# Attention before a mixture of experts on one core: the first pair of heads assembled by 0/1 matmuls, seven PSUM banks in rotation, the first four pairs worked by halves of the queries, and embeddings moved into the loop

## The chip, the core and the metric

The kernel runs on one core of a Trainium2 chip. A core has a matrix engine (TensorE, PE in the profile, with its weight loads as PEld), VectorE (DVE), ScalarE (ACT), GpSimd (POOL), and queues that issue transfers for its 16 DMA engines; here nearly all go through SyncE (SP). Each engine works its own instructions in order and waits on semaphores for the others. SBUF is the on-chip memory of 128 partitions, PSUM the accumulators of PE: eight banks of 128 x 512 four-byte numbers. The metric is the time of one execution on the device in microseconds (us), lower is better. A time shown for a kernel is the median of its runs.

## The reference

Input is `x` of 4 batches, 1024 tokens and 256 channels, in 16 heads of 16. What matters here is the attention:

```python
q_mag, k_mag = softplus(x @ wq.T), softplus(x @ wk.T)          # by head
q_embed = [q_mag * cos(qp), q_mag * sin(qp)]                   # 32 numbers for each token and head
k_embed = [k_mag * cos(kp), k_mag * sin(kp)]                   # kp: position angles + a bias for each head and channel
scores  = q_embed @ k_embed.T / sqrt(16)
out     = softmax(scores) @ v                                  # then @ wo.T
x       = layernorm(x + out)
x       = layernorm(x + moe(x))                                # 8 experts, the best 2 for each token
```

## The kernel before, in words

**Units.** The heads are cut into two groups `f` of eight, and worked by pairs of heads: 8 pairs for each batch, 32 in all, numbered through as `u`. A pair has eight steps, one for each tile of 128 keys, so there are 256 steps in the loop (L970 to L1018). "Pair 4" below is the first pair of group 1 of batch 0, at step 32.

**A step.** For the pair in work it makes the key scores `st` (keys on partitions, queries along the row) for both heads and all 1024 queries, four matmuls into two PSUM tiles of two banks (`key_scores`, L728); adds minus the query's maximum by four matmuls of two rows with ones (L743); takes exponentials into `pt` on ACT, two instructions of 128 x 1024 (L750); and multiplies the exponentials of the step before by the values, 16 matmuls into `av` (L764). Column 16 of the values is one, so `av` holds the sums too. For the next pair it makes four score tiles `s` the other way round (queries on partitions; `score_half`, L692 to L705) and DVE takes each one's row maximum into `nm`. A pair needs 32 of these. In step 6 of a pair the next pair's maxima are split in two parts (`max_parts`, L711 to L713, DVE), in step 7 they are turned into rows (`max_rows`, L719: four transposes on PE, a copy `mt` on ACT, L721). Extra work is set beside the steps by the table `todo`.

**Embeddings.** `embedding` (L350 to L416) makes 512 tokens of q or k for one group: two matmuls, softplus in three ACT instructions, two products with a table of cosines and sines, and a split of each product into a rounded part and the rest (`parts`, fp32r and its remainder), so that a score from both parts is as good as fp32. The fast form does products and remainders on DVE and the copies on ACT; the slow form does them on POOL (L390 to L405) and reads its table from DRAM. The result goes to DRAM in four writes (L413), because a pair's score matmul wants it in another order of partitions: 32 rows of q part 1, part 1, part 2, part 2 against k part 1, part 2, part 1, part 2, for one head. `load_qk` (L418 to L436) reads it back so: 12 transfers of a pair, four of q and two of k for each of the two heads.

**Tables.** `tab0` holds the angles' cosines and sines (`cs`) and the key table of group 0 (`kt0`). The key table of group 1 is made of `cs` by `second_key_table` (L225 to L235: four ACT copies with a scale, two POOL sums) and stored to DRAM for later batches and for group 1.

**Buffers.** The pool `big` has three buffers of 16 KB a partition: `twice` (weights, read until `once` has copied them), `tab0`, and the pairs' `qk`, which take these over when they are free. The pool tag `parts` has two buffers. `bank()` hands out PSUM: in the loop three single banks, before the loop and in the tail five in rotation, the three and one of the two banks of each `st` tile:

```python
free_banks[0] = (free_banks[0] + 1) % 5
if free_banks[0] > 2:
    return ps_st.tile([P, 2, HS], F32, tag="st", name=name)[:, 0, :]
```

**Before the loop** (L908 to L967, an order written out by hand): the fast embeddings of group 0 in halves of the tokens (k0, q0, k1, q1), each written and loaded back as pair 0 (q's through POOL's queue); the values of group 0; the load of pair 1; table stores; then all 32 score tiles of pair 0, with the two q embeddings of group 1, the values of group 1 and the second key table among them; `max_parts`, `max_rows`. In the loop, step 0 holds eight scores of pair 1 after its exponentials, every later step four; the two k embeddings of group 1 start in steps 2 and 4. At the start of a pair's first step the pair after the next is loaded.

Every SP transfer and every engine's order is as the program gives it; what waits for what follows from the tiles: an instruction waits for the last readers of a buffer that its tile takes over.

## Time and profile before

| | us |
|---|---|
| median of 3 runs (1452.09, 1455.23, 1455.70) | 1455.23 |
| profiled execution | 1455.47 |
| its span, first to last instruction | 1453.6 |
| start of the first exponentials of step 0 | 62.12 |
| steps 0 to 31 (to pair 4's first exponentials, 186.41) | 124.29 |
| PE busy from 0 to 62.12 | 40.91 |
| PE busy from 62.12 to 186.41 | 123.77 |
| PE busy from 186.41 to 1110 (923.59) | 904.29 |
| PE busy from 1110 to 1160 (the attention's tail) | 17.31 |
| PE busy from 1160 to the end (293.60, experts) | 281.41 |

A line of the profile names the engine, the line of the kernel, the operation and the tiles (output <- inputs), and in square brackets how long the engine had been idle and what ended that. Matmul ends are modelled, so a start-to-start distance says more than a duration. "PEclk" and the column after POOL in a table by windows is the clock that the chip granted to PE, 1.00 being full.

### The profile page before, as it was taken

The numbers are of one execution on the slowest core, as the hardware profiler recorded it, in microseconds if no ns is written. First come the engines' busy times: TensorE is split into PE (matmuls) and PEld (weight loads), VectorE is DVE, ScalarE is ACT, GpSimd is POOL, SyncE is SP. The second block draws the span as 40 slices with busy tenths as digits, with TensorE's granted clock in tenths as the row PEclk, the third lists the DMA queues.
The fourth block names the chain that finished last, engine by engine and source line by source line (L and its number), as shares of the span: only waits on it lengthen the run. The fifth ranks groups of instructions, "written<-read, shape, count | busy, mean of one in ns | idle before, by whom it ended". The sixth has DMA issues, their size and how long they took to land. (4 is left out here: it accounts for less than half of the span.)

```text
span 1453.6 us, 24361 instructions
## 1 busy us (share of the span) xinstructions
PE 1367.7 (94%) x9314; PEld 859.4 (59%) x9314; DVE 921.3 (63%) x1990; ACT 727.5 (50%) x944; POOL 411.2 (28%) x436
## 2 busy tenths in 40 slices
PE   5899999999999999999999999999996399999996
PEld 3455555655665565555555555555543277777775
DVE  7767766667877766787767677887644433333334
ACT  5365666565566556546674654655553122222221
POOL 5640043340002637000064530000210414444542
PEclk8899999999999999999999999999998599999998
DMA  7956367373444646454465352224210436433211
GB/s 240 261 177 173 100 188 205 87 228 107 126 120 113 213 133 180 121 151 102 129 185 181 105 176 74 63 63 118 90 64 0 139 112 212 115 120 131 73 44 43
DMA packets 107315, 191.23 MB, mean 132 GB/s; under 512 B 19633, under 2 KB 56178, under 8 KB 107072
## 3 DMA queue, kind: packets, MB, share of 16 engines
q1 hardware_dynamic: 96192, 167.80, 39.7%
q0 software_dynamic: 9888, 20.01, 4.5%
q10 hardware_dynamic: 1120, 1.87, 0.4%
q8 instruction: 73, 1.20, 0.4%
q14 instruction: 42, 0.34, 0.1%
HBM read 119.32 MB, written 73.63 MB: 133 GB/s over the span
## 5 line engine op out<-in xcount | busy, mean ns | idle before, releaser
L705 DVE TENSOR_REDUCE nm<-s 128x1 f32<-128x512 f32 x1024 | 644.8, 684 | 230.4 <-PE s L701 212.6
L750 ACT ACTIVATE pt<-st 128x1024 f32<-128x1024 f32 x512 | 496.3, 1021 | 393.7 <-PE st L743 378.9
L701 PE MATMUL s<-qk 128*128 128x512 f32 x1024 | 391.5, 441 | 25.6 <-DVE nm L705 14.5
L728 PE MATMUL st<-qk 128*128 128x512 f32 x1024 | 308.4, 401 | 3.5 <-ACT pt L750 3.4
L764 PE MATMUL av<-pt,va 128*32 128x256 f32 x4096 | 275.5, 386 | 0.5 <-ACT pt L750 0.5
L701 PEld LDWEIGHTS s<-qk 128*128 128x128 f32 x1024 | 180.2, 191 | 138.3 <-DVE nm L705 62.4
L728 PEld LDWEIGHTS st<-qk 128*128 128x128 f32 x1024 | 183.3, 189 | 67.1 <-ACT pt L750 32.7
L764 PEld LDWEIGHTS av<-pt,va 128*32 128x32 f32 x4096 | 107.1, 109 | 107.8 <-issue 62.4
L646 POOL DMA_INDIRECT slots_in<-held,scatter_idx x64 | 62.7, 980 | 304.4 <-DVE scatter_idx L644 226.4
L390 POOL TENSOR_TENSOR soft_q<-y_q,soft_q 128x512 f32<-128x512 f32 x14 | 17.9, 1282 | 447.3 <-ACT soft_q L386 447.2
L1249 PE MATMUL op<-w,h 128*128 128x256 f32 x640 | 144.1, 379 | 0.0
L1230 PE MATMUL hp<-slots_t,w 128*128 128x320 f32 x512 | 139.9, 434 | 0.0
L743 PE MATMUL st<-mt,ones_r 2*128 2x512 f32 x1024 | 129.6, 495 | 0.7 <-ACT mt L721 0.7
L1249 PEld LDWEIGHTS op<-w,h 128*128 128x128 f32 x640 | 119.4, 190 | 15.9
L1230 PEld LDWEIGHTS hp<-slots_t,w 128*128 128x128 f32 x512 | 97.7, 191 | 40.0 <-ACT slots_t L1083 0.3
L743 PEld LDWEIGHTS st<-mt,ones_r 2*128 2x128 f32 x1024 | 49.0, 181 | 89.5 <-issue 88.1
L1237 ACT ACTIVATE h<-hp,b_sb 128x640 f32<-128x640 f32 x64 | 50.8, 794 | 86.6 <-PE hp L1230 73.3
L1264 DVE TENSOR_TENSOR o<-op,b_sb 128x256 f32<-128x256 f32 x35 | 14.9, 425 | 93.3 <-PE op L1249 88.9
L1265 ACT ACTIVATE o<-o,w 128x256 f32<-128x256 f32 x35 | 17.8, 507 | 103.1 <-issue 71.9
L1267 POOL DMA_INDIRECT y_rank<-o,rows x35 | 35.9, 1025 | 98.4 <-ACT slots_t L1083 42.2
L1191 POOL DMA_INDIRECT out_dram<-row,rows x40 | 41.0, 1025 | 44.6 <-DVE row L1146 14.3
L396 POOL TENSOR_TENSOR e_k<-soft_k,tab_k 128x512 f32<-128x512 f32 x28 | 35.4, 1286 | 46.3 <-DMA tab_k<-table 45.8
(210 smaller groups left out, 1030.6 us busy)
## 6 DMA issues: line engine op xcount, KB each, us to landing
qk<-embed_q SPq DMA_DIRECT2D x248, 128.0 KB
qk<-embed_k SPq DMA_DIRECT2D x124, 256.0 KB
embed_k<-parts_k SPq DMA_DIRECT2D x64, 256.0 KB
w<-in_w_dram SPq DMA_DIRECT2D x16, 1024.0 KB
embed_q<-parts_q SPq DMA_DIRECT2D x56, 256.0 KB
y_rank<-zero SPq DMA_DIRECT2D x8, 1024.0 KB
tab_k<-table SPq DMA_DIRECT2D x14, 512.0 KB
tab_q<-table SPq DMA_DIRECT2D x12, 512.0 KB
```

Of the source, the lines that this page charges most:

```text
L646: nc.gpsimd.indirect_dma_start(out=scatter_views[2 * t + k], out_offset=bass.IndirectOffsetOnAxis(ap=scatter_idx[:, k, t : t + 1], axis=0) ...
L701: nc.tensor.matmul(ps, qk[:, 2 * h, lo : lo + P], qk[:, 2 * h + 1, j * HS : (j + 1) * HS], start=True, stop=True,)
L705: nc.vector.tensor_reduce(nms[u][:, j, i, s : s + 1], ps, AX.X, ALU.max, negate=True)
L728: nc.tensor.matmul(ps[:, f, :], qk[:, 2 * h + 1, c * P : (c + 1) * P], qk[:, 2 * h, f * HS : (f + 1) * HS], start=True, stop=False,)
L743: nc.tensor.matmul(tiles[h][:, f, :], ones_r[rows, :], mts[u][rows, :], start=False, stop=True,)
L750: nc.scalar.activation(pt, tiles[h], AF.Exp)
L764: nc.tensor.matmul(av[32 * s : 32 * (s + 1), cols], va[f][:, c, 2 * p + h, :], pt[h][:, s // 2, cols], start=(c == 0 and n == 0), stop=(c ...
L1191: nc.gpsimd.indirect_dma_start(out=out_views[t], out_offset=bass.IndirectOffsetOnAxis(ap=to[:, 0, t : t + 1], axis=0), in_=row[:, t, :], i ...
L1230: nc.tensor.matmul(ps[:, i, 0:half], w1_sb[:, k, c * P : (c + 1) * P], s_t[:, k, i * half : (i + 1) * half], start=(k == 0), stop=(k == KC ...
L1237: nc.scalar.activation(h_t[:, c, :].rearrange("p (i n) -> p i n", i=2), ps[:, :, 0:half], AF.Gelu, bias=b1_sb[:, e, c : c + 1],)
L1249: nc.tensor.matmul(ps, h_t[:, c, t * P : (t + 1) * P], w2_sb[:, c, :], start=(c == 0), stop=(c == HC - 1),)
L1267: nc.gpsimd.indirect_dma_start(out=y_views[e * ST + t], out_offset=bass.IndirectOffsetOnAxis(ap=to[:, 1, t : t + 1], axis=0), in_=o_sb, in ...
```

## The change

1. *Rows by matmul.* POOL makes `picks`, matrices of zeros and ones. `move_first` puts pair 0's rows in place with them: for q and k, each head and each half of the tokens, four matmuls that add both parts into their places in one PSUM tile, and an ACT copy into `qk_0`. `load_qk` for pair 0 is gone; the writes of the embeddings to DRAM stay, all on SP. The k1 and q1 parts lie in buffers of `pt`; q1 is made in the slow form.
2. *Seven banks.* Rotating work takes the three single banks and both banks of each `st` tile.
3. *Halves.* The four pairs of batch 0, group 0 are worked as eight units of four steps, each for half of the queries; a step then takes two tiles of keys for 512 queries. Before the loop only the 16 scores of the first half are made. A list `ahead` spreads the scores of later units: 6 in step 0, 5 in each of steps 1 to 18, then 4. `max_parts` and `max_rows` come once for each unit, and so do `av`'s copy and its six collecting transfers.
4. *Staged embeddings.* All four embeddings of batch 0, group 1 start in the loop, in steps 3, 7, 11 and 15, with products, split and writes in the steps after. Values of group 1: one half before the loop, one in step 5. The second key table is made in pieces in steps 0, 1, 8 and 9, in buffers of `parts` instead of `pt`. Pair 4's load moves from step 16 to step 19. `nm` has three buffers instead of two.

```diff
+        picks = p1.tile([P, 2, 2, 13, HD], F32R, tag="os", name="picks")
+        for h in range(2):
+            pick = p2.tile([P, 2, 13, HD], F32, tag="y", name=f"pick_{h}")
+            nc.gpsimd.memset(pick, 0.0)
+            for w, (first, apart) in enumerate(((5, 2), (3, 4))):
+                blocks = pick[:, w, first : first + apart + 1 : apart, :]
+                nc.gpsimd.affine_select(
+                    out=blocks, in_=blocks, compare_op=ALU.not_equal, fill=1.0, base=-h,
+                    pattern=[[0, 2], [-FH, HD]], channel_multiplier=1,
+                )
+            nc.gpsimd.tensor_copy(picks[:, h], pick)
...
         def second_key_table(h):
 
             cols = halves[h]
-            a = p4.tile([P, 2, HS], F32, tag="pt", name=f"kta_{h}")
-            kt = p4.tile([P, 2, HS], F32, tag="pt", name=f"kt_{h}")
+            both = p2.tile([P, 2, 2, HS], F32, tag="parts", name=f"kt_{h}")
+            a, kt = both[:, 0], both[:, 1]
             for i, c in enumerate((nb4, sb4)):
                 nc.scalar.activation(a[:, i, :], cs[:, 1 - i, cols], AF.Copy, scale=c[:, 1:2])
                 nc.scalar.activation(kt[:, i, :], cs[:, i, cols], AF.Copy, scale=cb4[:, 1:2])
-            for i in range(2):
                 nc.gpsimd.tensor_tensor(kt[:, i, :], kt[:, i, :], a[:, i, :], ALU.add)
+                if i == 0:
+                    yield
...
-                free_banks[0] = (free_banks[0] + 1) % 5
-                if free_banks[0] > 2:
-                    return ps_st.tile([P, 2, HS], F32, tag="st", name=name)[:, 0, :]
+                free_banks[0] = (free_banks[0] + 1) % 7
+                n = free_banks[0] - 3
+                if n >= 0:
+                    if n % 2 == 0:
+                        two_banks[0] = ps_st.tile([P, 2, HS], F32, tag="st", name=name)
+                    return two_banks[0][:, n % 2, :]
...
+            if apart:
+                parts = [
+                    p4.tile([P, 2, HS], F32R, tag="pt", name=f"parts_{name}_{p}") for p in range(2)
+                ]
+            else:
+                both = p2.tile([P, 2, 2, HS], F32R, tag="parts", name=f"parts_{name}")
+                parts = [both[:, 0], both[:, 1]]
             for i in range(2):
                 if fast:
-                    nc.scalar.copy(parts[:, 0, i, :], e[:, i, :])
+                    nc.scalar.copy(parts[0][:, i, :], e[:, i, :])
                 else:
-                    nc.gpsimd.tensor_copy(parts[:, 0, i, :], e[:, i, :])
+                    nc.gpsimd.tensor_copy(parts[0][:, i, :], e[:, i, :])
             for i in range(2):
-                fine.tensor_tensor(
-                    parts[:, 1, i, :], e[:, i, :], parts[:, 0, i, :], ALU.subtract
-                )
+                fine.tensor_tensor(parts[1][:, i, :], e[:, i, :], parts[0][:, i, :], ALU.subtract)
+            if made is not None:
+                made[w, h] = parts
...
-            by = nc.gpsimd if fast and w == "q" else nc.sync
             for p in range(2):
                 for i in range(2):
-                    by.dma_start(
+                    nc.sync.dma_start(
                         to[2 * p + i, :, :, cols].rearrange("d m s -> (d m) s"),
-                        parts.bitcast(F32)[:, p, i, :],
+                        parts[p].bitcast(F32)[:, i, :],
...
+        def move_first(w, cols, parts):
+
+
+            if 0 not in qks:
+                qks[0] = big.tile([P, 4, S], F32R, tag="big", name="qk_0")
+            k = w == "k"
+            for h in range(2):
+                ps = bank(f"rows_{w}_{h}_{cols.start}", True)
+                for p in range(2):
+                    for c in range(2):
+
+                        at = c + (2 if k else 4) * p
+                        first = (3 if k else 5) - at
+                        nc.tensor.matmul(
+                            ps,
+                            picks[:, h, int(k), first : first + 8, :].rearrange("p b d -> p (b d)"),
+                            parts[p][:, c, :],
+                            start=(p == 0 and c == 0),
+                            stop=(p == 1 and c == 1),
+                        )
+                yield
+                nc.scalar.copy(qks[0][:, 2 * h + k, cols], ps)
...
+        units = []
+        starts, lasting = [], []
+        for i in range(B * NU):
+            for h in range(2) if i < NU // NF else (None,):
+                starts.append(starts[-1] + lasting[-1] if units else 0)
+                units.append((i, *divmod(i // (NU // NF), NF), i % (NU // NF), h))
+                lasting.append(NT if h is None else NT // 2)
+        NS = starts[-1] + lasting[-1]
+        step_of = [(w, c) for w in range(len(units)) for c in range(lasting[w])]
...
+            i, _, _, _, half = units[w]
+            qk = qks[i]
+
+            i, s = divmod(k, 4 if half is None else 2)
+            h = s % 2
+            if w not in nms:
+                nms[w] = small.tile([P, 2, 4, 4], F32, tag="nm", name=f"nm_{w}", bufs=3)
+            lo = HS * (s // 2 if half is None else half) + P * i
+            ps = bank(f"s_{w}_{k}_{j}", rotate)
...
+                h, q, k = (t, x, c) if half is None else (x, half, 2 * c + t)
...
+                        to, k, e = slice(n * DIM, (n + 1) * DIM), c, pt[h][:, q]
+                        e = e[:, to]
...
+                        to, k, e = slice(0, DIM), 2 * c + n, pt[n][:, h]
...
-                if b == 0 and n > 1:
-                    staged(0, ((0, 2), (0, 4))[n - 2], 2, embedding, 0, 1, w, h)
+                if b == 0:
+                    staged(0, ((0, 3), (0, 7), (1, 3), (1, 7))[n], 1, embedding, 0, 1, w, h)
...
+        ahead = [[] for _ in range(NS)]
+        items, due, may = [], [], []
+        for w in range(1, len(units)):
+            rows = range(16 if units[w][4] is None else 8)
+            items += [(w, k, j) for k in rows for j in range(2)]
+            due.append((starts[w] - 2, len(items)))
+
+            before = [starts[v] for v in range(w) if units[v][0] == units[w][0] - 1]
+            may.append((max(0, min(before, default=1) - 1), len(items)))
+        given = 0
+        for n in range(NS):
+            n_items = max([-((given - i) // (d - n + 1)) for d, i in due if d >= n], default=0)
+            most = max(i for first, i in may if first <= n)
+            ahead[n] = items[given : min(given + n_items, most)]
+            given += len(ahead[n])
...
+                    0, 0, w, h, fast=(w, h) != ("q", 1), tab=cs if w == "q" else kt0,
+                    pauses=(KC - 1,), rotate=True, apart=h == 1, made=made,
...
+            for work in (q0, k0, q0, k0, k1, q0, q1):
                 run(work)
+            mk0, mq0 = moving("k", 0), moving("q", 0)
+            key_table(1)
+            for work in (k1, mk0, mq0, mk0, mq0, mk0, mq0, mk0, mq0):
                 run(work)
+            for i in range(2):
+                score_half(0, 2 * i, 0, True)
+            for work in (k1, q1, k0, q0):
                 run(work)
+            for i in range(2, 4):
+                score_half(0, 2 * i, 0, True)
+            values(0, 0, 0, rotate=True)
+            for i in range(4):
+                score_half(0, 2 * i + 1, 0, True)
+            mk1 = moving("k", 1)
+            for work in (mk1, mk1, mk1, mk1, k1):
                 run(work)
+            for i in range(4):
+                score_half(0, 2 * i, 1, True)
+            values(0, 0, 1, rotate=True)
+            for i in range(4):
+                score_half(0, 2 * i + 1, 1, True)
+            run(q1)
+            values(0, 1, 0, rotate=True)
+            max_parts(0)
+            max_rows(0, rotate=True)
+            mq1 = moving("q", 1)
+            for work in (mq1, mq1, mq1, mq1, q1):
+                run(work)
...
-            works = [embedding(0, 1, "q", h, tab=cs, pauses=(0, 1)) for h in range(2)]
-            vals = [values_in_two(0, 1, h) for h in range(2)]
-            beside = {n: (run, works[0]) for n in (3, 5, 6, 11, 17)}
-            beside |= {n: (run, vals[i]) for n, i in ((8, 0), (10, 0), (14, 1), (16, 1))}
-            beside |= {n: (second_key_table, h) for n, h in ((1, 0), (12, 1))}
-            beside |= {n: (run, works[1]) for n in (20, 22, 23)}
...
+        for h in range(2):
+            pieces = second_key_table(h)
+            for c in range(2):
+                at(0, h, c, run, pieces)
+        at(0, 0, 5, values, 0, 1, 1)
...
+                if n % NT == 0 and n != 2 * NT or n == 2 * NT + 3:
+                    i = n // NT + 2
+                    if i < B * NU:
+                        load_qk(i)
...
+                items = [(score_half, *x) for x in ahead[n]]
+                first, third, fourth, rest = items[:2], items[2:3], items[3:4], items[4:]
+                if third_last:
+                    third, fourth = [], third + fourth
...
+                if n + 2 in starts:
+                    max_parts(starts.index(n + 2))
+                if n + 1 in starts:
+                    max_rows(starts.index(n + 1))
```

## The prediction

> **What bounds the kernel now.** First the page: engine shares, and the slices of TensorE (PE) with the clock that it was granted.
>
> ```profile
> PE 1367.7 (94%) x9314; PEld 859.4 (59%) x9314; DVE 921.3 (63%) x1990; ACT 727.5 (50%) x944; POOL 411.2 (28%) x436
> ...
> PE   5899999999999999999999999999996399999996
> ...
> PEclk8899999999999999999999999999998599999998
> ```
>
> PE is full from the third slice of 36 us up to the tail of the attention. Time can be won by less PE work, or in the two places where PE is not full: the start, and about 1,110 to 1,160 us, which the change touches only through the bank order. So next the start, by windows (busy time of PE, PEld, DVE, ACT, POOL; then granted clock, share of the DMA engines, GB/s):
>
> ```profile
> 20.00:30.00 10.00, 1.95 (x18) 1.76 (x16) 9.93 (x19) 7.69 (x14) 6.74 (x14) 0.76 0.79 266
> 30.00:40.00 10.00, 7.71 (x13) 3.70 (x13) 5.00 (x12) 2.43 (x5) 5.60 (x11) 0.56 0.90 298
> ...
> 50.00:60.00 10.00, 6.05 (x18) 2.79 (x16) 8.62 (x15) 2.44 (x4) 9.79 (x10) 0.97 0.67 249
> 60.00:70.00 10.00, 9.32 (x25) 5.14 (x24) 6.79 (x12) 2.52 (x3) 1.54 (x2) 0.52 1.02 291
> ```
>
> PE is nearly empty from 20 to 30 us; from 50 to 60 DVE leads. The waits from 0 to 90 us (total, times, longest) say on what:
>
> ```profile
> DVE nm L705 <- PE s L701: 18.7, 17, 3.3
> ...
> PE s L701 <- DMA qk<-embed_q: 9.9, 2, 8.5
> ```
>
> The timeline places them:
>
> ```profile
> 30.41 0.77 PE L701 MATMUL s<-qk 128*128 128x512 f32 x1 [8.46 <-DMA qk<-embed_q]
> ...
> 59.18 1.03 PE L719 MATMUL mp<-ident,m 128*128 128x128 f32 x4 [3.13 <-DVE m L713]
> 60.25 0.59 ACT L721 CAST mt<-mp 128x512 fp32r<-128x512 f32 x1 [6.19 <-PE mp L719]
> ...
> 62.12 1.94 ACT L750 ACTIVATE pt<-st 128x1024 f32<-128x1024 f32 x2 [1.28 <-PE st L743]
> ...
> 106.89 1.94 ACT L750 ACTIVATE pt<-st 128x1024 f32<-128x1024 f32 x2 [1.55 <-PE st L743]
> 110.38 1.94 ACT L750 ACTIVATE pt<-st 128x1024 f32<-128x1024 f32 x2 [1.55 <-PE st L743]
> ```
>
> The first score waits 8.46 us for the embedding's way through DRAM; 32 scores and maxima follow; the first exponentials of the loop start at 62.12 us. Then a step takes 3.49 us (110.38 - 106.89), with PE never idle. Steps 0 to 31, the part that the change rebuilds, start at 62.12 and end where pair 4's first exponentials start, 186.41: 124.29 us.
>
> **The way up to the first exponentials.** Removed: 24 loads of pair 0, and the eight POOL issues of q's writes, which move to SP behind k's. No score waits for those. Added on PE: 32 matmuls of the size of a score (0.23 us apart at full clock in the steady steps), about 7.4 us in all, half of them where PE now stands idle; on ACT eight copies of 128x512 at 0.59 (L345's and L721's rows). POOL's masks (two fills, four selects, two copies) lie in its idle time between 12.7 and 19.4 us. I followed the new order of instructions with these rows: k's first split ends at 20.8, 1.5 us later than now, because its Abs waits for DVE's copy of an x tile that lies in the same PSUM tile (seven banks are three tiles and two tiles of two banks, and a wait is by tile); q's ends at 22.1; rows are copied at 22.7, 23.4, 25.2 and 26.1; the first score is at 26.2 instead of 30.4. Sixteen maxima at 0.62 to 0.68 instead of 32, with the half embeddings, the values and the shared tiles between them, put the last at 44.1; maxima in parts 1.8 (L711 to L713 from 57.33 to 59.13) to 45.9; transposes, copy and ones as now (59.18 to 62.12, 2.9), with waits for a shared tile and the last four row matmuls between: 51.3 at full clock. **Gain: 62.1 - 51.3 = 10.8 us.** Bounds: 14 if the shared tiles cost nothing (first exponentials at 48), 6 if one cold stretch as that from 25 to 39 us comes back.
>
> **Steps 0 to 31.** The measured 124.29 is 32 x 3.49 = 111.68, plus 7.65 for the cold start (steps of 9.36, 4.51 and 4.25), one embedding 1.90, four maxima transposes of 0.39 and four x transposes of 0.38: 124.3. After: 111.68, plus 20 more scores than four a step (6 in step 0, 5 in each of steps 1 to 18) at 0.23 = 4.60, four embeddings 7.60, one half of values 1.87, eight maxima transposes 3.12, x transposes 1.52: **130.4, so 6.1 us more.** The halves themselves are free: per four steps of a half as many key, ones and value matmuls as before. Without new waits the change is worth 10.8 - 6.1 = 4.7 us. The collects double to 12 small transfers a pair on SP, and ACT has one copy of `avs` (0.6) more a pair, beside 55 to 60% busy; nothing for these.
>
> **The new wait.** SP works its queue in order, so what one load waits for delays all behind it. Now:
>
> ```profile
> 62.17 2.29 SPq L432 DMA_DIRECT2D qk<-embed_q  x4
> 64.50 1.41 SPq L436 DMA_DIRECT2D qk<-embed_k  x2
> ...
> 69.75 0.39 SPq L357 DMA_DIRECT2D tab_k<-table  x1
> ```
>
> Pair 2's load (12 transfers, issued in step 0) goes at once, and a table load follows. In the change the second key table is computed in steps 0, 1, 8 and 9, so the angles stay live until step 9, and pair 2's load gets pair 0's buffer instead of theirs. It then waits for the last key scores of pair 0, in step 7. With steps 0 to 2 at 4.0, 3 at 5.9, 4 at 3.7, 5 at 5.6 and 6 at 3.7, these end about 81.3. Behind it on SP stand the store of the key table's first half, the table load of the embedding that step 3 began, six collects, and that embedding's writes. Nothing computes the embedding without its table:
>
> ```profile
> 81.78 2.53 POOL L396 TENSOR_TENSOR e_k<-soft_k,tab_k 128x512 f32<-128x512 f32 x2
> 84.26 1.17 POOL L403 CAST parts_k<-e_k 128x512 fp32r<-128x512 f32 x2
> 85.39 2.53 POOL L405 TENSOR_TENSOR parts_k<-e_k,parts_k 128x512 fp32r<-128x512 f32 x2
> ```
>
> That is 6.2 us (81.78 to 87.92). And the second half of the key table, ACT work of step 8 ahead of step 9's exponentials, now lies in the two `parts` buffers in turn, so it waits until this embedding's four writes have landed. From 81.3: 12 issues of pair 2, now 95.27 to 101.28, then the store, 6.7; the table landed 5 to 6 us later, behind two MB (a later quiet load landed 6.6 for its first six transfers and 10.8 for all); POOL 6.2; writes 2.0 to 2.3, now landing so when DMA is quiet: 20 to 21.4. ACT is freed at 101.5 to 102.7, having wanted to go on at about 90.7: **11 to 12 us**. What is queued behind it: step 9's exponentials, then PE's step 10, which needs the score tiles that these read. PE runs ahead by some 2 us of other work (values of step 8, two scores), then stands.
>
> For the clock that follows, first the row (columns as above):
>
> ```profile
> 59.30:62.70 3.40, 2.73 (x11) 1.64 (x11) 0.25 (x1) 1.17 (x2) 2.24 (x2) 0.50 1.05 403
> 62.70:66.10 3.40, 3.40 (x7) 1.44 (x5) 3.40 (x7) 1.35 (x2) 0.00 (x0) 0.50 1.04 252
> 66.10:69.50 3.40, 3.40 (x8) 2.44 (x8) 3.03 (x6) 0.00 (x0) 0.00 (x0) 0.50 0.96 248
> ```
>
> After 3 us of idle PE the clock was 0.50 for 10.2 us although PE had work from 59.2 on. [...] By the row it is 10.2, so 5.1 lost. [...] Stall 11.5 - 2 + 2.5 = 12.0. [...]
>
> Other loads that I followed are in time: pair 1 landed at 57.7 at the latest and wanted at 61; pair 2's first six transfers at 81.3 + 6.6 = 87.9, wanted at 90.6; pair 3 two steps early; pair 4 waits for POOL's four embeddings in a row and lands about 4 us before it is wanted. If that cover is gone, each microsecond late is one of PE. After step 31 the order is as before; seven banks may move the tail by 1 us either way.
>
> **Sum.** -10.8 + 6.1 + 12.0 = +7.3. The profiled execution took 1455.47 (span 1453.6 and 1.9 around it), so 1462.8; the median of 1455.23 is 0.2 below. I say **1463 us**. 0.3%, or 4.4 us, is about what a measurement of this kernel can tell from no change.
>
> **Rivals.**
> - *The wait is covered.* One mechanism: the embedding's writes are landed when ACT comes to the second table in step 8. That needs 81.3 to 90.7, 9.4 us, in place of 20: not with POOL's 6.2 and 2 for the writes after a table load queued behind pair 2. But if the first half of the loop runs later than I think relative to step 7's keys, or the table overtakes pair 2 in the DMA engines, it shrinks to 3 to 5. No stall: 1455.5 - 4.7 = 1450.8, faster; it decides below a stall of 4.7 us. Chance 0.23, half of it faster by over 0.3%.
> - *The start doesn't gain.* DVE and shared tiles stretch it: first exponentials at 56 (gain 6) with the stall as worked: 1467.6. For it: DVE is busy 9.93 of 10 us from 20 to 30. Against: half the maxima are gone. Chance 0.15.
> - *A second stall or the row's cold clock*: pair 4's load late by 4 us, or 5.1 for the clock: 1467 to 1472. Chance 0.12.
> - *The start is quicker* (48 instead of 51.3) with the stall: 1459.5, or with half of it 1454. Chance 0.1.
>
> The forecast itself, 1459.6 to 1467: 0.40. Faster: 0.12 + 0.04 = 0.16; within 0.3%: 0.11 + 0.06 and a little of the forecast's lower edge, 0.21; slower 0.63. The range leaves out the clearest covered case and the worst of the second stalls: 1450 to 1470.
>
> **What would show it.** First exponentials near 51 us; row copies on ACT from about 22.5; the steps 0 to 2 near 4.0 us; SP's load of pair 2 issued about 30 us after the loop starts; ACT waiting at the second table's Copy for writes of `embed_q`, about 11 us, with PE idle and a clock of 0.50 after it; pair 4 starting near 194. Wrong if that wait is under 5 us, or if the first exponentials come before 47 or after 56.

## The result, and the profile after

The changed kernel is slower, and by more than was forecast.

| | before | after |
|---|---|---|
| median, us | 1455.97 (6 runs, 1452.09 to 1459.96) | 1473.22 (6 runs, 1466.43 to 1475.70) |
| ratio to before | | 1.0106, 95% interval 1.0076 to 1.0136 |
| profiled execution / span, us | 1455.47 / 1453.6 | 1466.43 / 1464.7 |
| first exponentials of step 0 | 62.12 | 51.99 |
| steps 0 to 31 | 124.29 | 150.66 |
| pair 4's first exponentials | 186.41 | 202.65 |
| last pair's first exponentials | 1077.58 | 1090.00 |

The first trace of the changed kernel fell on a quick execution: four of the six took 1473 to 1476. It shows the loss's place all the same: 10.1 us were won before the loop and 26.4 given back in steps 0 to 31. (Of the 16.2 us by which pair 4 is late, 3.8 are gone at the last pair; between the two the trace of before has two windows of half clock, at 772.7 and 854.6 us, and the trace after has one, at 522.1.)

The page after, engine shares and slices:

```profile
PE 1375.4 (94%) x9362; PEld 865.3 (59%) x9362; DVE 918.7 (63%) x1997; ACT 733.1 (50%) x959; POOL 407.3 (28%) x427
...
PE   6869999999999999999999999999996399999997
...
PEclk9989999999999999999999999999999599999999
```

PE's first slice is a little fuller (6 against 5 before) and the second as full (8), but the third, from 73 to 110 us, now has a hole (6 against 9), and the clock drops there (the 8 in PEclk). The start by windows (columns as in the prediction):

```profile
20.00:30.00 10.00, 6.66 (x24) 3.75 (x23) 9.40 (x17) 7.81 (x14) 0.00 (x0) 1.00 0.68 259
30.00:40.00 10.00, 6.25 (x31) 4.33 (x30) 6.25 (x10) 2.59 (x5) 8.62 (x14) 1.00 0.38 145
40.00:50.00 10.00, 7.81 (x52) 6.54 (x51) 4.46 (x13) 2.66 (x5) 0.00 (x0) 1.00 0.81 284
50.00:60.00 10.00, 9.84 (x66) 5.65 (x68) 9.06 (x15) 7.06 (x10) 2.37 (x2) 1.00 0.78 181
```

PE has work between 20 and 30 us (6.66 against 1.95), and the loop runs from 52 us. The waits from 0 to 110 us:

```profile
POOL e_q L415 <- DMA tab_q<-table: 28.7, 2, 24.9
...
ACT kt L246 <- DMA embed_q<-parts_q: 13.0, 1, 13.0
...
PE st L801 <- ACT pt L822: 11.8, 1, 11.8
```

They form one chain, which the timelines of SP, POOL, ACT and PE show in that order:

```profile
59.26 0.60 SPq L290 DMA_DIRECT2D rb_sb<-in_router_b_dram  x1
82.31 1.99 SPq L480 DMA_DIRECT2D qk<-embed_q  x4
...
89.50 0.41 SPq L376 DMA_DIRECT2D tab_q<-table  x1
...
99.28 3.32 SPq L437 DMA_DIRECT2D embed_q<-parts_q  x4
```

```profile
96.21 2.48 POOL L415 TENSOR_TENSOR e_q<-soft_q,tab_q 128x512 f32<-128x512 f32 x2 [24.90 <-DMA tab_q<-table]
```

```profile
89.35 1.92 ACT L822 ACTIVATE pt<-st 128x1024 f32<-128x1024 f32 x2
...
104.48 0.72 ACT L246 ACTIVATE kt<-tab,nb 128x512 f32<-128x512 f32 x1 [12.95 <-DMA embed_q<-parts_q]
...
105.72 1.92 ACT L822 ACTIVATE pt<-st 128x1024 f32<-128x1024 f32 x2
```

```profile
106.78 1.22 PE L801 MATMUL st<-qk 128*128 128x512 f32 x2 [11.85 <-ACT pt L822]
```

SP stands from 60 to 82.31 us for pair 0's buffer, issues pair 2's load, then the table at 89.50. The table lands at 96.2, POOL computes, the writes land at 104.48, 22.2 us after pair 2's load went. ACT has waited 12.95 us for them, with step 9's exponentials behind it, and PE 11.85. It is the chain that the prediction describes.

### The profile page after: what moved, and what is told of

It is laid out like the page before. It is cut to its first block, busy times and chain, and to the rows that moved or that the text cites. A ratio compares the mean times of both kernels' runs of the same rounds, so it can differ in the third digit from the quotient of the medians.

```text
span 1464.7 us, 24497 instructions
## 1 busy us (share of the span) xinstructions
PE 1375.4 (94%) x9362; PEld 865.3 (59%) x9362; DVE 918.7 (63%) x1997; ACT 733.1 (50%) x959; POOL 407.3 (28%) x427
## 3 DMA queue, kind: packets, MB, share of 16 engines
q1 hardware_dynamic: 97792, 169.90, 39.7%
q8 instruction: 74, 1.21, 0.4%
## 5 line engine op out<-in xcount | busy, mean ns | idle before, releaser
L761 PE MATMUL s<-qk 128*128 128x512 f32 x1022 | 386.1, 437 | 18.8 <-DVE nm L765 17.4
L509 DVE TENSOR_TENSOR held<-po,held 128x512 f32<-128x512 f32 x32 | 22.1, 691 | 41.6 <-PE po L501 41.6
```

Of the source, the lines that this page charges most:

```text
L761: nc.tensor.matmul(ps, qk[:, 2 * h, lo : lo + P], qk[:, 2 * h + 1, j * HS : (j + 1) * HS], start=True, stop=True,)
```

## Experiments

Unless it says otherwise, each is the changed kernel with the edit shown. "Start" is the first exponentials of step 0, "loop" steps 0 to 31, both from the profiled execution. Medians differ between chips (the kernel before: 1450.39 us on one and 1457.40 on another), so ratios to the kernel before on the same chip are compared.

| run | ratio to before, 95% interval | median, us | start | loop | pair 4 |
|---|---|---|---|---|---|
| before | 1 | | 62.12 | 124.29 | 186.41 |
| changed | 1.0106 (1.0076 to 1.0136) | 1473.22 | 51.99 | 150.66 | 202.65 |
| e8 changed again | 1.0132 (1.0107 to 1.0156) | 1469.85 | 56.50 | 151.50 | 208.00 |
| e1 pair 2's load later | 1.0017 (1.0004 to 1.0029) | 1458.26 | 55.17 | 140.11 | 195.28 |
| e2 key table early | 1.0032 (1.0017 to 1.0047) | 1459.87 | 53.89 | 138.12 | 192.01 |
| e3 PE kept warm | 1.0112 (1.0091 to 1.0133) | 1471.61 | 54.95 | 150.97 | 205.92 |
| e4 five banks | 1.0065 (1.0044 to 1.0086) | 1464.47 | 46.01 | 150.72 | 196.73 |
| e5 five banks, key table early | 0.9957 (0.9940 to 0.9973) | 1447.09 | 47.68 | 136.28 | 183.96 |
| e6 and table loads ahead | 0.9964 (0.9952 to 0.9976) | 1446.95 | 46.52 | 136.86 | 183.38 |
| e9 and table loads first | 0.9952 (0.9936 to 0.9968) | 1443.35 | 44.15 | 135.72 | 179.87 |
| e10 e5 with rows by load | 1.0029 (1.0019 to 1.0039) | 1455.85 | 55.38 | 138.97 | 194.35 |
| e7 before with rows by matmul | 1.0039 (1.0023 to 1.0054) | 1457.31 | 69.18 | 122.29 | 191.47 |
| e11 e9 with whole pairs | 1.0119 (1.0095 to 1.0143) | 1469.44 | 65.86 | 140.69 | 206.55 |
| e12 and loads early | 0.9957 (0.9932 to 0.9982) | 1449.69 | 55.80 | 128.27 | 184.07 |

### The wait at the second key table

```diff
+                if n == NT:
+                    load_qk(2)
-                if n % NT == 0 and n != 2 * NT or n == 2 * NT + 3:
+                if n % NT == 0 and n not in (0, 2 * NT) or n == 2 * NT + 3:
```

> The changed kernel with one edit: pair 2's load is issued at the start of step 8 instead of step 0, so that on SP it stands behind the table load, the collects and the writes of the embedding begun in step 3; its buffer is still pair 0's, free after step 7. My theory (SP's queue in order carries pair 2's wait on to the embedding's table, and from there through POOL and the writes to the second key table): ACT waits at the second table for less than 1 us, PE keeps its clock of 1.00 there, pair 4's first exponentials come at 185 to 188 instead of 202.65, and the time is 15 to 17 us under the changed kernel, about 1456. Rival (POOL's six instructions or the collects are late by themselves, whatever SP does): the wait at the second table stays above 6 us and the time within 8 us of the changed kernel.

The edit changes only the place of pair 2's load on SP; it keeps pair 0's buffer, and was issued at 85.47. ACT's timeline at the same place:

```profile
94.38 0.37 ACT L852 COPY avs<-av 128x256 f32<-128x256 f32 x1
94.62 0.75 ACT L246 ACTIVATE kt<-tab,nb 128x512 f32<-128x512 f32 x1
...
96.29 1.94 ACT L822 ACTIVATE pt<-st 128x1024 f32<-128x1024 f32 x2 [0.32 <-PE st L815]
```

The second table follows the copy at once; the wait of 12.95 us is gone, and the clock was 1.00 there. So it was SP's order: POOL and the writes are fast enough when the table isn't queued behind pair 2. The loop fell from about 151 to 140.1, and the ratio from 1.0106 and 1.0132 to 1.0017. It did not come down to the 185 to 188 expected of pair 4: steps 14 and 15 took 6.95 and 8.81 us, and the start was 55.17. In step 14 PE waited 2.46 us for DVE, whose three small instructions on the maxima took 0.43, 1.22 and 1.19 us while POOL worked on the third embedding, and half clock followed (124.3 to 131.1 us). What DVE was late with is taken up below.

```diff
-                at(0, h, c, run, pieces)
+                at(0, 0, 2 * h + c, run, pieces)
...
+                if n == 4:
+                    load_qk(2)
```

> The changed kernel with the second key table made in steps 0, 1, 2 and 3 and pair 2's load at step 4, where it gets the angles' buffer. If the wait of the second table is the whole loss: no wait of ACT for writes of the embedding, pair 4 at 184 to 187, time 1453 to 1457, within 2 us of the run with the later load. Rival (another buffer of the same two is late next: the embedding's parts wait for the store of the second table): a stall of 3 us or more in steps 4 to 8 on POOL alone, which PE doesn't see until pair 4's load, and pair 4 at 190 or later.

The wait is gone in this way too; pair 4 at 192.01 lies between the two expectations, and the ratios of the two runs overlap. Steps 10 and 11 took 5.75 and 7.62 us where my terms make 3.7 and 6.0. (The expectation of a later run says 4.1 and 5.6; it sets the transposes of the maxima into step 10, and the trace has them in step 11.) In step 10 PE waited 1.64 us for DVE, and a window of half clock followed in step 11.

### The clock after the stall

In the trace of the changed kernel, windows of about 3.4 us (columns as in the prediction):

```profile
98.90:102.30 3.40, 0.00 (x0) 0.00 (x0) 0.00 (x0) 0.00 (x0) 3.40 (x5) 0.50 0.53 204
102.30:105.70 3.40, 0.00 (x0) 0.00 (x0) 0.00 (x0) 1.22 (x2) 1.17 (x1) 0.50 0.80 210
105.70:109.10 3.40, 2.32 (x6) 1.82 (x6) 0.64 (x1) 3.16 (x5) 1.81 (x2) 0.50 0.14 54
109.10:112.55 3.45, 3.45 (x23) 1.21 (x22) 0.74 (x2) 1.94 (x2) 3.45 (x5) 0.50 0.62 160
112.55:115.96 3.41, 3.41 (x8) 2.17 (x7) 2.83 (x4) 0.00 (x0) 3.30 (x3) 0.50 0.99 250
```

PE resumed at 106.78 and got its full clock at 115.96: 9.2 us of half clock, near the row of before (10.2). What it costs, 2.5 us in the forecast, was tried:

```diff
+                if n == 10:
+                    warm = ps_3.tile([P, 512], F32, tag="bank", name="warm")
+                    for i in range(48):
+                        nc.tensor.matmul(
+                            warm, qks[1][:, 0, 0:P], qks[1][:, 1, 0:HS], start=True, stop=True
+                        )
```

> The changed kernel with 48 added matmuls of a score's size ahead of step 10's key scores, in the stall, whose results nothing reads; the stall of ACT stays as it is. It prices the clock alone. By the changed kernel's trace (half clock for 9.2 us of work after the stall): PE keeps 1.00 or gets it back at once, steps 9 to 11 give back 3.5 to 5 us, pair 4 comes at 198 to 199.5 instead of 202.65. If the clock costs about 2.5 us, as I forecast, pair 4 comes at 200 or later. If the clock costs nothing, or the added matmuls outlast the stall, no gain.

PE's timeline with the added matmuls:

```profile
98.17 11.17 PE L1103 MATMUL warm<-qk 128*128 128x512 f32 x48 [0.32 <-DVE nm L765]
110.14 0.74 PE L801 MATMUL st<-qk 128*128 128x512 f32 x2 [0.80 <-ACT pt L822]
...
118.36 0.50 PE L761 MATMUL s<-qk 128*128 128x512 f32 x1 [2.71 <-DVE nm L765]
```

The clock stayed at 1.00 through the stall to 120.4, and nothing was won: steps 8 to 11 took 34.7 us against 34.4 in the first trace, and pair 4 came at 205.92. I had expected 3.5 to 5 back. Step 9 did fall, from 4.81 to 3.46, but in step 10 PE waited 2.71 us for DVE, and a window of half clock followed in step 11, which took 7.61 us instead of 5.95. So holding the clock up through the stall won nothing: DVE was the next limit behind it, and half clock came back behind the wait of 2.71 us for it.

### What DVE was late with

In step 10 the maxima of the next half are split by three DVE instructions on 8 or 16 numbers a partition. Before the loop, with POOL idle, they took 0.17, 0.18 and 0.19 us; in step 10 of the warmed run 0.70, 1.21 and 1.19. Over the first trace of the changed kernel the copy among them took at most 0.19 us in the 26 places where no POOL instruction on data ran beside it, and 0.80 in the mean, 1.23 at most, in the 10 where one did. So the second embedding, late on POOL, slows DVE. Two edits tried to have POOL done in time, both on the kernel with the early key table and five banks (below). The first lets `embedding` pause once after its table load:

```diff
-                    staged(0, ((0, 3), (0, 7), (1, 3), (1, 7))[n], 1, embedding, 0, 1, w, h)
+                    pieces = embedding(0, 1, w, h, ahead_table=True)
+                    for c in (1, 3, 4, 5):
+                        at(0, n // 2, 4 * (n % 2) + c, run, pieces)
```

> The run before this with each staged embedding's table load issued two steps ahead of the embedding. It tests what is late in steps 10 and 11 (5.75 and 7.62 us where 4.1 and 5.6 were worked out). My theory: POOL's late products meet DVE's three small instructions on the maxima, which take up to 1.2 us each beside a running POOL instruction and 0.2 alone; with the table early POOL is done before them: step 10 at 4.1 to 4.6, step 11 at 5.6 to 6.2, pair 4 some 3 us earlier. Rival (the scores' banks or pair 2's load are what is late there): steps 10 and 11 within 0.5 us of the run before this.

Here the edit missed: the second table load was still issued at 84.33, as SP stood from 59 to 70 us at the store of the second key table, and POOL waited 4.10 us for it. Step 10 took 6.00 us, 0.6 more than in the run before it, where DVE's three instructions took 0.27, 1.22 and 0.19 us; step 11 took the 6.0 of my terms in both. DVE and POOL in step 10 of this run:

```profile
94.36 0.88 DVE L780 TENSOR_TENSOR nm<-nm 128x8 f32<-128x8 f32 x1
95.28 1.20 DVE L781 CAST m<-nm 128x16 fp32r<-128x16 f32 x1
96.52 0.19 DVE L782 TENSOR_TENSOR m<-nm,m 128x16 f32<-128x16 f32 x1
```

```profile
93.93 2.51 POOL L429 TENSOR_TENSOR parts_q<-e_q,parts_q 128x512 fp32r<-128x512 f32 x2
```

The first DVE instruction ends at 95.24, about when the first of POOL's two does; the second at 96.48, POOL's second at 96.44; the third, with POOL idle, takes 0.19. The second edit puts the table load ahead of that store:

```diff
-                    for c in (1, 3, 4, 5):
-                        at(0, n // 2, 4 * (n % 2) + c, run, pieces)
+                    c = 4 * n + 3
+                    for c in ((1, 2, 9, 13)[n], c, c + 1, c + 2):
+                        at(0, 0, c, run, pieces)
...
-                at(0, 0, 2 * h + c, run, pieces)
+                at(0, 0, ((0, 1), (2, 4))[h][c], run, pieces)
...
-                if n == 4:
+                if n == 5:
```

> Five banks, the second key table in steps 0, 1, 2 and 4, pair 2's load at step 5, and the table loads of the staged embeddings issued in steps 1, 2, 9 and 13, so that the second one stands on SP ahead of the second key table's store, on which SP stood still for 11 us in the run with the tables ahead (59.1 to 70.2). My theory (DVE's small instructions on the maxima are slow beside POOL): POOL is done with the second embedding before step 10's maxima, these take 0.2 us each, step 10 takes 4.1 to 4.6 instead of 5.4 to 6.0, step 3 takes 5.6 to 6.2 instead of 7.17, pair 4 at 179 to 182 and 1442 to 1446. Rival (scores, banks or pair 2's load set step 10): step 10 stays above 5.2.

The same places in its trace:

```profile
92.52 0.16 DVE L780 TENSOR_TENSOR nm<-nm 128x8 f32<-128x8 f32 x1
92.72 0.18 DVE L781 CAST m<-nm 128x16 fp32r<-128x16 f32 x1
92.94 0.19 DVE L782 TENSOR_TENSOR m<-nm,m 128x16 f32<-128x16 f32 x1
```

```profile
88.03 2.52 POOL L429 TENSOR_TENSOR parts_q<-e_q,parts_q 128x512 fp32r<-128x512 f32 x2
```

POOL ends at 90.55, the maxima take 0.53 us together, and step 10 takes 4.28 instead of 6.00, as expected. Step 3, which no longer holds a piece of the key table, took 5.93 instead of 7.17. Step 2 gave 1.4 us of this back (5.78 instead of 4.38): PE waited 1.81 us for a transfer, by the order of the scores the load of pair 1, which the earlier loop wants earlier. This is the best kernel of the study: 0.9952 of before (0.9936 to 0.9968). Its pair 4 is 3.5 us earlier than in the run before it, but only 1.1 of that lies in the loop. The other 2.4 lie in the start, which has full clock throughout in this trace and a window of half clock in the other (28.4 to 31.8 us). Its ratio is not distinguishable from that run's, so the edit is shown in its steps and not in the time. In the rows of the run before this one, ends of DVE's and POOL's instructions coincide (96.48 and 96.44 us). The reductions, which read PSUM here, take the same beside POOL as without it: none of the 1024 in the first trace of the changed kernel took over 0.70 us.

### Seven banks

```diff
-                free_banks[0] = (free_banks[0] + 1) % 7
-                n = free_banks[0] - 3
-                if n >= 0:
-                    if n % 2 == 0:
-                        two_banks[0] = ps_st.tile([P, 2, HS], F32, tag="st", name=name)
-                    return two_banks[0][:, n % 2, :]
+                free_banks[0] = (free_banks[0] + 1) % 5
+                if free_banks[0] > 2:
+                    return ps_st.tile([P, 2, HS], F32, tag="st", name=name)[:, 0, :]
```

> The changed kernel with the rotation of five banks as in the kernel before, so no two works share a tile of two banks. It prices the seven banks. My theory: the shared tiles cost as much as the two more banks bring, so the first exponentials come between 50.5 and 53 instead of 51.99, the stall of about 12 us stays, and the time is within 2 us of the changed kernel. If the seven banks carry the gain of the start: first exponentials at 55 or later. If the shared tiles cost what I bounded them with: 48 to 49.

I was wrong on this: with two banks fewer the loop begins at 46.01 us, 6 earlier than in the first trace and 8 to 10 earlier than in the four others with the same start, although a window of half clock fell into this start too (27.6 to 31.0); the ratio fell to 1.0065. PE's waits for the maxima, from 26 us to the loop, in the changed kernel:

```profile
PEld s L761 <- DVE nm L765: 7.6, 5, 1.9
PE s L761 <- DVE nm L765: 5.5, 5, 1.5
```

With five banks:

```profile
PEld s L758 <- DVE nm L762: 1.6, 2, 1.2
```

A wait is by tile: work in the second bank of a tile waits for the reading of the first. One line of the changed kernel shows this by itself, a score that shares its tile with values and waits 0.68 us for ACT's copy of them, of which it uses nothing:

```profile
32.31 0.50 PE L761 MATMUL vp<-qk 128*128 128x512 f32 x1 [0.68 <-ACT va L364]
```

So with two scores in a tile PE writes one bank and DVE reads it, in turn. The stall behind is the same (steps 8 and 9: 16.37 and 4.81). Both repairs together:

> The changed kernel with both repairs: five banks in rotation, and the second key table in steps 0 to 3 with pair 2's load at step 4. If the two losses add: first exponentials 46 to 49 (46.0 with five banks alone), steps 0 to 31 in 138 as with the table moved, pair 4 at 184 to 187, time 1451 to 1455, so 0 to 5 us under the kernel before. If the shared tiles' cost is only moved into the loop: pair 4 at 190 to 192 and 1458 to 1460, as with the table alone.

They add: start 47.68, loop 136.28, pair 4 at 183.96, and the kernel is faster than before, 0.9957 (0.9940 to 0.9973), by 5.6 us in the medians, a little over the 0 to 5 expected.

### The start in another execution

> The changed kernel itself, for a second trace beside the others on one chip. Its first trace (first exponentials 51.99, full clock through the start, 1466.43) was shorter than its median of 1473.22. My theory: in most executions single windows of half clock fall into the start, as in the two runs with the same start (55.17 and 53.89), so the first exponentials come at 53.5 to 56 and pair 4 at 204 to 208. Rival: the start is as in the first trace, and the stall is longer (over 14 us at the second table).

The start differs with the execution as expected, a little more so: 56.50. Its granted clock fell to half from 36.3 to 39.7 and from 43.1 to 46.6. Over 10 us PE was no less busy there than in the first trace, which kept full clock (7.39 against 6.25 us from 30 to 40). By stretches of 3.4 us, each of the two falls follows one in which PE was busy for less than half of the time (1.58 and 1.47 us):

```profile
32.90:36.30 3.40, 1.58 (x6) 0.96 (x6) 1.66 (x4) 0.58 (x1) 3.32 (x4) 1.00 0.16 62
36.30:39.70 3.40, 3.40 (x9) 2.31 (x8) 1.07 (x2) 0.70 (x2) 3.40 (x5) 0.50 0.54 198
39.70:43.10 3.40, 1.47 (x6) 0.77 (x6) 1.98 (x3) 0.47 (x1) 1.30 (x8) 1.00 0.62 231
43.10:46.60 3.50, 3.50 (x18) 3.40 (x18) 0.69 (x1) 0.24 (x1) 0.00 (x0) 0.51 1.03 383
```

The stall is about as long as in the first trace (step 8: 17.31 against 16.37), so the rival, a longer stall, isn't what makes the median.

### Rows and halves

```diff
             def moving(w, h):
-                return move_first(w, halves[h], made[w, h])
...
+                for m in range(2):
+                    rows = embed[0, 0, w][:, :, m, cols].rearrange("k d s -> (k d) s")
+                    for i in range(4 if w == "q" else 0):
+                        lo = 32 * (i // 2)
+                        nc.gpsimd.dma_start(
+                            raw[32 * i : 32 * (i + 1), 2 * m, cols], rows[lo : lo + 32, :]
+                        )
+                    for i in range(2 if w == "k" else 0):
+                        nc.sync.dma_start(raw[64 * i : 64 * (i + 1), 2 * m + 1, cols], rows)
```

> The run with both repairs (five banks, key table early) with pair 0's rows loaded back from DRAM as in the kernel before (q's by POOL's queue) in place of the row matmuls and their copies; the 0/1 matrices are still made. It prices the first part of the change inside the repaired kernel. If the way through DRAM is on the start's path: first score at 30 to 31 us instead of 26.5, first exponentials 4 to 8 us later than 46 to 48, time 4 to 8 us over that run. If DVE's maxima and the values hide it: first exponentials within 2 us and no difference in time.

```profile
32.20 2.05 PE L758 MATMUL s<-qk 128*128 128x512 f32 x4 [12.82 <-DMA qk<-embed_q]
```

On the kernel with both repairs, the way through DRAM makes the first score late: it waits 12.82 us, and the later halves wait again (3.85 and 1.49 us). The start, whose order is adapted to the loads, is 7.7 us longer than with the matmuls, half clock behind the long wait included (23.0 to 36.6), and the ratio is 1.0029 instead of 0.9957. That is about 10 us and over the 4 to 8 expected; 2.5 of it lie in steps 10 and 11 (13.89 us against 11.39). So the rows are worth what was expected or a little more, once banks and queue don't take it back.

The first part of the change alone, on the kernel before, in an order of the start that I wrote for it (k1 and q1 as in the changed kernel, the 32 scores with all other works beside them):

```diff
+                                one = moving(them[1], 1)
+                                them = (one,) * 4
...
-            load_qk(0, halves[0], "q", nc.gpsimd)
```

> The kernel before with the first part of the change alone: pair 0's rows by matmuls with zeros and ones, k1 and q1 as in the changed kernel, five banks, whole pairs with all 32 scores before the loop, the other works of the start beside these. If the rows are the gain and the halves only move work into the loop: first exponentials at 55 to 58 instead of 62.12, steps 0 to 31 in 122 to 125, pair 4 at 178 to 182, time 4 to 8 us under the kernel before. If DVE's 32 maxima set the start whatever the rows do: first exponentials at 60 or later and the time within 2 us of the kernel before.

Neither expectation came: the start took 69.18. Its first score came at 26.76, 3.7 us earlier than in the kernel before, but two windows of half clock (35.2 to 38.6, 42.0 to 45.4) and the works between the scores used that up. The loop was 2.0 us shorter. This order is mine, so the run doesn't price that part.

To price the halves, the best kernel was given whole pairs, with all 32 scores before the loop:

```diff
-            for h in range(2) if i < NU // NF else (None,):
+            for h in (None,):
...
+            for j in range(2):
+                for i in range(4):
+                    for h in range(2):
+                        score_half(0, 4 * i + 2 + h, j, True)
```

> The best run so far (five banks, tables first) with the halves undone: all pairs are whole, all 32 scores of pair 0 stand before the loop, and the spreading list gives pair 1's 32 scores to steps 0 to 6 (5, 5, 5, 5, 4, 4, 4). It prices the third part of the change. By the forecast's terms: the start longer by 16 maxima at 0.62, so 10 us (first exponentials at 53 to 56 instead of 44.2); the loop shorter by 16 scores at 0.23 and four transposes at 0.39, so 5 us (steps 0 to 31 in 129 to 131 instead of 135.7); pair 4 at 183 to 186, time 4 to 6 us over that run. If the halves' gain is given back in the loop: pair 4 within 2 us of 179.9.

It didn't price them: pair 1's scores are wanted from step 0 and pair 2's from step 7, and PE waited 6.9 and 7.9 us for their loads. The halves also hide loads. With these earlier:

```diff
-            once("k", 1)
-            once("q", 1)
-            load_qk(1)
...
+            once("k", 1)
+            once("q", 1)
+            load_qk(1)
             for j in range(2):
                 for i in range(4):
...
-                if n == 5:
+                if n == 3:
                     load_qk(2)
```

> The run with whole pairs again, with its two late loads moved: pair 1's is issued ahead of pair 0's last 16 scores (its PE wait of 6.9 us stood ahead of step 0), pair 2's at step 3 (waits of 7.9 and 2.1 us stood in step 7), the second key table in steps 0 to 3. With both covered only the halves' own price is left: first exponentials at 53 to 58, steps 0 to 31 in 129 to 133, pair 4 at 184 to 189, time 1446 to 1452, so 3 to 8 us over the best run with halves. If the halves are worth nothing: pair 4 at 178 to 182. If pair 2's load is still late: step 6 or 7 above 8 us.

Start 55.80 and pair 4 at 184.07 are within what was expected, the loop at 128.27 a little under it. Against the best kernel the halves make the start 11.7 us shorter (this run's ends in 3 us of half clock, the best kernel's has none) and the loop 7.5 longer: 4.2 us by the traces. But this trace is of an execution 3.6 us over its median, and the two ratios, 0.9957 and 0.9952, don't tell the kernels apart. The 3 to 8 us expected in the time did not come; by the time alone the halves may be worth nothing.

## Why the prediction was wrong

The direction, the place and the mechanism of the wait were right. The sum was too small, because the terms for the start, for steps 0 to 31 and above all for the stall were mis-sized, and the range ended 3 us too low.

- *The start, "62.1 - 51.3 = 10.8 us".* 10.1 in the first trace, as worked out "at full clock". In the four other traces of the same start (55.17, 53.89, 54.95, 56.50) it was 5.6 to 8.2, with single windows of half clock. The row of before (25 to 39 us at half clock) gave me the lower bound of 6; I took the other end. So the second rival ("the start doesn't gain", 56) came about in number in most traces, and in part for its reason: the shared tiles did stretch the start, the rest was clock.
- *"Follow ... the shared tile".* The wait for shared tiles was in my timeline, but its price was not: I bounded the start without it by 48 us, and the four traces with five banks and the same order gave 44.2 to 47.7.
- *Steps 0 to 31, "130.4".* Outside the stall they took about 3 us more: 150.66 less the 34.39 of steps 8 to 11 is 116.3, and my terms for the same steps make 113.2 (130.4 less three times 3.72 and 6.01 for steps 8 to 11). Of this, 2.3 us lie in steps 2, 6, 14 and 18, in which the next half's maxima are split: 4.26 to 4.39 us instead of 3.72. In step 6 DVE splits them ahead of the last reductions, with POOL idle, and a score's weights wait for it:

```profile
82.38 0.19 PEld L761 LDWEIGHTS s<-qk 128*128 128x128 f32 x1 [0.58 <-DVE nm L765]
```

With four scores in the step (steps 22 and 30) the same splitting cost nothing (3.50). So "the halves themselves are free" counted PE's work and left out DVE's.
- *"Stall 11.5 - 2 + 2.5 = 12.0".* This term failed most: it cost 17.2, as steps 8 to 11 took 34.39 instead of 17.17. ACT's wait was 12.95 for my 11.5 (the table took 6.7 from its issue, against 5 to 6). PE stood for 11.85 of it, so it ran ahead by 1.1 and not by 2. What follows the wait I called clock and took at 2.5. No run shows this term: what followed the wait cost the other 5.4. The half clock lasted 9.2 us, but the run kept warm shows that DVE's maxima beside POOL hold step 10 nearly as long (6.85 us against 7.26). I had missed that neighbour altogether, and had its row in hand: the 1.8 us that I took for the three maxima instructions from 57.33 on had POOL beside them, and alone they take 0.54.
- *The sum.* With the typical start, -7.0 + 6.1 + 17.2 + 3 = +19 at pair 4 (+16.2 and +21.6 in the two traces of the changed kernel), and +17 in the medians; forecast +7.3.
- *Rivals.* "The wait is covered" (1450.8) is answered by the run with the later load: the wait gone, the kernel still at 1.0017, because of the maxima (its step 14) and the seven banks. "A second stall": pair 4's load was not late; DVE was.

## What to carry to other kernels

When a load is moved or gets another buffer, follow what stands behind it on its queue to the last instruction of another engine that waits for it; here a load that waited for its buffer held up the exponentials by 12.95 us. Banks taken from a shared tile are not free banks, since a wait is by tile: from 26 us to the loop, weight loads of scores waited 7.6 us for maxima with the shared tiles and 1.6 with five banks. And before a small DVE instruction's duration is read from a row, look whether POOL ran beside it: here a copy took up to 1.23 us so, and 0.19 alone.

## What the runs showed of the hardware

- Half clock lasted 9.2 us after PE took up work again behind the stall, 10.2 us in the start of the kernel before, although PE was busy, by its modelled ends, in the whole of the last two rows each time (3.45 of 3.45 and 3.41 of 3.41 us; 3.40 of 3.40 twice).
- In the traces before and after, the shortest stretch of half clock lasted 3.41 us. Ahead of each of the 12 falls to half clock in the two, PE was busy for 2.01 us or less of 3.41; ahead of each of the ten returns, for 3.22 us or more of 3.41. Other stretches of 3.41 us with 1.74 to 2.00 us of PE busy brought no fall (from 1103.8 us before; from 30.6, 37.5, 40.9 and 1116.1 after), and two with PE busy throughout brought no return (from 62.7 us before, from 109.1 after). What decides in these cases stays open.
- A DVE copy of 16 numbers a partition took up to 1.23 us beside POOL and 0.19 alone, in the traces before and after.
